# A fused convolution block of three stages: the third stage opens in an order of its own, and the taps come from eight products

## The chip, the core and the metric

One core of a Trainium2 chip. It has a matrix engine (PE, with its weight loads listed apart as PEld), a vector engine (DVE), a scalar engine for activations (ACT), GpSimd (POOL, used here for memsets and for issuing DMAs) and a queue processor that issues DMAs (SP). The program writes the order of instructions for all five by hand. The time is device microseconds of one launch; lower is better.

## What is computed

The input is x, 16 images of 192 channels and 64 × 64 pixels, f32. Layer 0 is a gated block; layer 1 is a dynamic depthwise convolution. Cut to what matters here:

```
h     = layernorm over channels (x)
p, g  = split(conv1x1(h, in_proj))                    # 192 -> 2 x 192
p     = depthwise3x3(p)
mixed = (four directional scans of p + depthwise3x3(p)) * sigmoid(g)
mixed = gelu(batchnorm(mixed))                        # mean and variance over all 16 images
x     = x + conv1x1(mixed, out_proj)                  # "out-projection", residual
h2    = layernorm over channels (x)                   # mean, variance, root
x     = x + conv1x1(gelu(conv1x1(h2, fc1)), fc2)      # 192 -> 768 -> 192
# layer 1, per image:
red   = relu(norm(mean over pixels(x) @ w1.T))        # 48 numbers
taps  = red @ w2.T + b2                               # 9 per channel, 4 of them kept by a causal mask
out   = depthwise3x3(x, taps) + bias
```

## The kernel before, in words

Stage 1 (up to about 640 us) normalises x and projects it into p and g, which go to DRAM. Stage 2 (up to about 1323 us) walks over 24 groups of 8 channels: depthwise, scans and gate, in SBUF; each finished group is stored to a DRAM tensor `mixed_d` (L707, one DMA on POOL's queue, 2 MB). The buffers for the groups take turns between `low`, `pg_o0` and `mid`. The last group lies in `mid`. Because the batch norm needs all 16 images, stage 3 can apply it only after the last group.

Stage 3 works on pairs of images, so that 64 channels of one image and 64 of the other fill 128 partitions: three "t" of 64 channels each. A pair is cut into 8 chunks of 512 pixels per image; there are 64 chunks in all. A chunk n goes through these functions:

- `load_y` (L209 to L231) reads mixed rows back for two chunks at a time: for chunks 0 and 1 into `y_low`, for chunks 2 to 7 of the first pair into parts of ximg1, the tile of the second pair's images, which isn't in use yet. With two queues it writes quarters of 64 KB (L231), with one queue larger pieces (L227).
- `unmix` (L847): three DVE transposes (`turn_back`, L239) into `mx`; `bn_gelu` (L853): batch norm and gelu on ACT, one instruction for the first two thirds (L855), one for the last (L856).
- `out_proj` (L877), for each t: four products with the last third of the channels ("quarters", L883, 64 × 64), then four with the first two thirds ("columns", L887, 128 × 64). `residual` (L890): two DVE instructions (L893) that add bias and x and write into the image tile ximg. At t = 1 and t = 2 it also adds up the channels' thirds for the mean: L897 and, by `sums`, four of L908.
- `mean` (L910, L916) turns these sums into a mean over channels by a product with a matrix of 1/192; `center` (L918, L923) subtracts it; `squares` (L927) squares on ACT (L930) and adds on DVE (L931, L908); a second `mean` makes the variance; `normalize` (L936) takes the root on ACT (L939, which needs a table load), warms up the gelu table (L941), inverts (L942) and multiplies (L943) on DVE.
- `first(n, k)` (L945), k = 0 to 2: a "hidden part", two slices of 128 hidden channels each, 24 matrix instructions a slice (L955), each slice followed by a gelu on ACT (L957). `second` (L960, by the helper `both` at L828) projects back; `final` (L969) adds.

The profile counts every f32 product as two matrix instructions with a weight load each. The matrix engine's output memory (PSUM) is laid out as two rotating tiles "f1" of two banks each, which the hidden slices, the out-projections and the means all share (in `products`, L858, a mean and an out-projection lie in two halves of the same tile), three banks "f2", and one bank "a".

When a pair is done, `pooled`, `squeeze` (L987) and `excite` (L997) make its taps. `excite` issues, for each of 3 t and 4 taps, one product for each image half (L1002, listed as L828 on the tile ps_k), and one add (L1004). The taps of pairs 0 to 6 are made between the third hidden part of a chunk and its out-projection; those of the last pair stand alone in the tail, before the last convolutions (`taps_on_diagonals`, `dynamic_last`).

The order: the loop at L1060 runs from n = -3, and in each turn touches chunk n + 3 (load, unmix, gelu), n + 2 (out-projection), n + 1 (mean to normalise), n (hidden parts) and n - 1 (the last of `second`, `final`). The first three turns have fewer members than the others. The tile pools matter as well: the pool `early` (L160), with constants, `dm` and `mid`, is closed at L795, and `k3` takes its place with ximg0 first and ximg1 behind it. With 12870 f32 per partition for each, ximg0 lies over the constants and a part of `mid`, ximg1 over the rest of `mid` and over `pg_o0`.

Of the kernel before, what the change touches and what calls it, by code (L numbers as in the profile page):

```python
# [21 lines left out]
F32 = mybir.dt.float32  # L22
AF = mybir.ActivationFunctionType
# [4 lines left out]
C = 192  # L28
HW = 64
NPIX = HW * HW  # L30
RW = HW + 2
CH = 512
HCH = CH // 2
# [22 lines left out]
def conv_block_kernel(ctx: ExitStack, tc: tile.TileContext, x, prm, w_in, w_out, w_fc1, b_fc1, w_fc2, w1, bn1, w2, out):  # L56
# [102 lines left out]

    early = ExitStack()  # L160
    ce = early.enter_context(tc.tile_pool(name="early", bufs=1))
    ones = ce.tile([128, 128], F32, tag="ones", name="ones")


# [7 lines left out]

    mats = [{"dm": ce.tile([128, 3, HW, GC], F32, tag=f"dm{i}", name=f"dm{i}")} for i in range(2)]
    mats[0]["lm"] = lm_even

    SB_ = 2 * 2 * C * BR
    mid = ce.tile([128, SB_], F32, tag="mid", name="mid")
    mats[1]["lm"] = mid[:, NPG:NPG + 5 * HW * (GC // 2)].rearrange("p (k m c) -> p k m c", k=5, m=HW)
    dev = mid[:, NPG + 5 * HW * (GC // 2):NPG + 5 * HW * (GC // 2) + 2 * C].rearrange("p (e c) -> p e c", e=2)
    lm_first = place.rearrange("p (k m c) -> p k m c", k=5, m=HW)  # L180
# [28 lines left out]
    def load_y(n, y, queues, ts=(0, 1, 2), last=32):  # L209

        p, c = divmod(n, NCH)
        for t, q, i, c0 in ((0, slice(0, 128), 0, 0), (1, slice(0, 128), 1, 0), (2, HALF[0], 0, 128), (2, HALF[1], 1, 128)):
            if t in ts:
                nq = (q.stop - q.start) // 32
                ih, i8 = divmod(2 * p + i, n_half)
                v = mixed_d[i8, c // 2, HALF[ih]].rearrange("w g e -> w (g e)")[:, c0 * BR:(c0 + 32 * nq) * BR]
                for wh in range(2):
                    vw = v[32 * wh:32 * wh + 32].rearrange("w (q e) -> q w e", q=nq)  # L220
                    qd, k = (q, wh) if t < 2 else (HALF[wh], i)
                    if last < 32:
                        for b, ncb in ((0, 32), (1, last)):
                            p0 = qd.start + 32 * b
                            queues[0].dma_start(y[p0:p0 + 32, t, k, 0:ncb * BR], vw[b, :, 0:ncb * BR])
                    elif len(queues) == 1:
                        queues[0].dma_start(y[qd, t, k], vw)  # L227
                    else:
                        for b in range(nq):
                            p0 = qd.start + 32 * b  # L230
                            queues[b % 2].dma_start(y[p0:p0 + 32, t, k], vw[b])  # L231
# [355 lines left out]
    with ExitStack() as stage:  # L587
# [100 lines left out]
        def gate(k):  # L688
            g, c = divmod(k, hp_)
            s = grp[g]  # L690
            blocks = lambda a: a.rearrange("p (n j) -> p n j", j=BR)
            for i in range(2):
                ch = c + hp_ * i

                o = s["pg"][:, :, 0, ch]
                nc.vector.tensor_mul(o, blocks(bst[k]["ps"][i]), blocks(bst[k]["sg"][i]))
                nc.vector.bn_stats(stats[:, g * GC + ch], o)
            bst[k].clear()
            if c == hp_ - 1:
                if g == NCG - 1:  # L700

                    for i in range(2):
                        for wh in range(2):
                            w0_ = 32 * wh
                            (nc.sync, nc.gpsimd)[wh].dma_start(y_low[2 * w0_ + 32:2 * w0_ + 64, 2, i, LASTC * BR:],
                                                              s["pg"][w0_:w0_ + 32, i * NB, 0].rearrange("p c j -> p (c j)"))
                nc.gpsimd.dma_start(mixed_d[:, :, :, g].rearrange("i b p e -> p (i b) e"),  # L707
                                    s["pg"][:, :, 0].rearrange("p n c j -> p n (c j)"))
                s.clear()


# [85 lines left out]


    n_img = 2
    ximg = [k3.tile([128, 3, HW + 1, RW], F32, tag=f"ximg{i}", name=f"ximg{i}") for i in range(n_img)]  # L800

    def border(xi):
        nc.gpsimd.memset(xi[:, :, 0:1], 0.0)
        nc.gpsimd.memset(xi[:, :, :, 0:1], 0.0)
        nc.gpsimd.memset(xi[:, :, :, RW - 1:RW], 0.0)
# [19 lines left out]
    def both(ps, w, rhs, start, stop):  # L825

        for i, q in enumerate(HALF):
            nc.tensor.matmul(ps[q], w(i), rhs(i), start=start, stop=stop)  # L828

    def img_of(n):  # L830
        r = 1 + (n % NCH) * CR
        return ximg[(n // NCH) % n_img][:, :, r:r + CR, 1:1 + HW]

    def rows(a):
        return a.rearrange("p (h w) -> p h w", w=HW)

    def load(n):
        if n >= 2:
            load_x2(n)
        st[n].update(x2=x2s[n % 2])  # L840
# [36 lines left out]
    def out_proj(n, t, ps):  # L877

        s = st[n]

        for wh, qr in enumerate(HALF):
            for i, q in enumerate(HALF):
                nc.tensor.matmul(ps[q, wh], wo2[qr, 64 * t:64 * t + 64], s["mx"][qr, 2, 256 * i:256 * i + 256],  # L883
                                 start=True, stop=False)
        for wh in range(2):
            for i, q in enumerate(HALF):
                nc.tensor.matmul(ps[q, wh].rearrange("p (r w) -> p r w", w=32), wo[:, 64 * t:64 * t + 64],  # L887
                                 cols(rows(s["mx"][:, i]))[:, :, wh], start=False, stop=True)

    def residual(n, t, ps):  # L890
        s, img = st[n], img_of(n)
        for wh in range(2):
            nc.vector.scalar_tensor_tensor(cols(img[:, t])[:, :, wh], ps[:, wh].rearrange("p (r w) -> p r w", w=32),  # L893
                                           pt3[:, t, OUTB:OUTB + 1], cols(rows(s["x2"][:, t]))[:, :, wh], ALU.add, ALU.add)
        if t == 1:
            s["sum"] = hp2.tile([128, 3, HCH], F32, tag="sm", name="sm", bufs=1)
            nc.vector.tensor_add(rows(s["sum"][:, 0:2].rearrange("p k n -> p (k n)")), img[:, 0], img[:, 1])  # L897
        if t == 2:
            sm = s["sum"]
            s["sm"] = [sm[:, j] for j in range(3)]  # L900
            sums(*(rows(sm[:, j]) for j in (0, 1, 2, 0, 1)), img[:, 2, 0:CR // 2], img[:, 2, CR // 2:CR])
# [8 lines left out]
    def mean(n, ps, what):  # L910


        s0, s1, sx = st[n][what]
        for k, kinds in enumerate(((s0, sx), (sx, s1))):
            for i, a in enumerate(kinds):
                nc.tensor.matmul(ps[HALF[i], k], mean64[HALF[k]], a[HALF[k]], start=True, stop=True)  # L916

    def center(n, pm):  # L918
        s, img = st[n], img_of(n)
# [76 lines left out]

    def excite(p):  # L997
        s = pst[p]
        pk = ps2.tile([128, 3, NTAP, 1], F32, tag="a", name="ps_k")
        for t in range(3):  # L1000
            for k in range(NTAP):
                both(pk[:, t, k], lambda i: w2t[:, k, 64 * t:64 * t + 64], lambda i: s["red"][:, i:i + 1], True, True)  # L1002
        taps = hp2.tile([128, 3, NTAP], F32, tag="taps", name="taps")
        nc.vector.tensor_add(taps, pk[:, :, :, 0], pt3[:, :, B2:B2 + NTAP])  # L1004
        s["taps"] = taps

    def dynamic(p, g, t):
# [42 lines left out]
    def at(f, n, *a):  # L1050
        if n is not None and 0 <= n < n_ch:
            f(n, *a)
# [4 lines left out]
        if pieces:  # L1057
            dynamic(*pieces.pop(0))

    for n in range(-3, n_ch + 1):  # L1060
        ended = (n - 1) // NCH if n >= NCH and (n - 1) % NCH == NCH - 1 else None
        if n + 5 < NCH and (n + 5) % 2 == 0:
            load_y(n + 5, ys[(n + 5) // 2], (nc.sync, nc.gpsimd) if n == -3 else (nc.gpsimd,))
        if n == -3:
            border(ximg[0])
        if n == 0:
            nc.vector.memset(pool2, 0.0)
        if n == NCH - 3:
            border(ximg[1])

        early_, late_ = (n + 3, None) if n != -1 else (None, 2)
        at(load, n + 3)
        at(unmix, early_)
        at(load_mixed, n + 4)
        at(first, n, 0)
        at(bn_gelu, early_)
        products(n, 0)
        piece()
        at(squares, n + 1)
        at(second, n - 1, NPS - 1)  # L1080
        at(final, n - 1)
        if ended is not None:
            pooled(ended)
        at(first, n, 1)
        products(n, 1)
        if ended is not None:
            squeeze(ended)
        at(second, n, 0)
# [9 lines left out]
        at(unmix, late_)  # L1098
        at(bn_gelu, late_)

    last = n_pairs - 1

# [61 lines left out]
```

## Time and profile before

| what | value |
|---|---|
| time before, median of 4 runs | 3756.06 us (3753.91 to 3762.54) |
| the profiled execution: time, span | 3753.91 us, 3752.1 us |
| PE, DVE, ACT busy, share of the span | 99%, 72%, 48% |
| first out-projection of stage 3 starts | 1330.71 us |
| first hidden part of chunk 0 starts | 1362.32 us |
| first hidden part of chunk 1 starts | 1397.44 us (chain of waits) |
| last projection ends, tail begins | 3710.4 us |

A busy share says little by itself: PE counts as busy also when it runs at half its clock, and a share is a mean over stages with different limits. The page has a row PEclk for the granted clock. Rows of groups give engine, operation, tiles written and read, shapes (partitions × elements), count, and idle time with what ended it; the timeline gives start and length in us. An "issue" as releaser means that the profile shows nothing that was waited for.

### The profile page before, as it was taken

The numbers are of one execution on the slowest core, as the hardware profiler recorded it, in microseconds if no ns is written. First come the engines' busy times: TensorE is split into PE (matmuls) and PEld (weight loads), VectorE is DVE, ScalarE is ACT, GpSimd is POOL, SyncE is SP. The second block draws the span as 40 slices with busy tenths as digits, with TensorE's granted clock in tenths as the row PEclk, the third lists the DMA queues.
The fourth block names the chain that finished last, engine by engine and source line by source line (L and its number), as shares of the span: only waits on it lengthen the run. The fifth ranks groups of instructions, "written<-read, shape, count | busy, mean of one in ns | idle before, by whom it ended". The sixth has DMA issues, their size and how long they took to land.

```text
span 3752.1 us, 71230 instructions
## 1 busy us (share of the span) xinstructions
PE 3696.8 (99%) x30252; PEld 1655.3 (44%) x30252; DVE 2716.5 (72%) x4260; ACT 1795.6 (48%) x1945; POOL 421.5 (11%) x683
## 2 busy tenths in 40 slices
PE   8999999999999979999999999999999999999998
PEld 5666656555555533333333333333333333333333
DVE  6887776999999965557756766666766776675763
ACT  3443434888888833334443434443443434443432
POOL 2334332101001020000000000000000000000000
PEclk9999999999999989999999999999999999999999
DMA  6899997999999940112222222222222221221212
GB/s 161 241 250 237 272 277 244 303 284 276 274 284 269 239 104 18 55 39 70 72 62 66 62 68 64 67 57 67 77 60 55 78 71 40 80 76 43 68 37 74
DMA packets 308429, 491.76 MB, mean 131 GB/s; under 512 B 46656, under 2 KB 202640, under 8 KB 308112
## 3 DMA queue, kind: packets, MB, share of 16 engines
q1 hardware_dynamic: 250064, 295.14, 29.8%
q0 software_dynamic: 57152, 190.94, 18.7%
q8 instruction: 239, 3.92, 0.4%
q10 hardware_dynamic: 896, 1.12, 0.1%
q14 instruction: 78, 0.64, 0.1%
HBM read 284.91 MB, written 197.92 MB: 129 GB/s over the span
## 4 chain that ended last, share of the span: by engine, by line
PE 97%; DVE 1%; DMA 1%; POOL 0%; issue 0%; ACT 0%; SPq 0%; ACTq 0%; DVEq 0%
PE ps_f L955 27%; PE ps_f L828 26%; PE ps_pj L512 13%; PE ps_l L662 11%; PE ps_d L618 7%; PE ps_o L887 5%; PE ps_xt L484 2%; PE ps_o L883 2%; PE ps_o L916 1%; DMA xa<-in_x_dram 1%; PE ps_k L828 0%; DVE v L653 0%; DVE v L655 0%; DMA ximg<-mixed_d 0%; PE ps_d L1038 0%
## 5 line engine op out<-in xcount | busy, mean ns | idle before, releaser
L957 ACT ACTIVATE gl<-ps_f,bf 128x1024 f32<-128x1024 f32 x384 | 427.9, 1114 | 1316.1 <-PE ps_f L955 1316.1
L955 PE MATMUL ps_f<-h,wf 64*64 64x512 f32 x9216 | 1036.0, 595 | 6.7 <-DVE h L943 6.6
L828 PE MATMUL ps_f<-gl,place 128*64 128x512 f32 x4608 | 1022.2, 592 | 0.0
L955 PEld LDWEIGHTS ps_f<-h,wf 64*64 64x64 f32 x9216 | 334.6, 133 | 693.8 <-issue 642.6
L828 PEld LDWEIGHTS ps_f<-gl,place 128*64 128x64 f32 x4608 | 334.2, 137 | 574.5 <-issue 533.4
L512 PE MATMUL ps_pj<-wi,xa 64*128 64x384 f32 x3072 | 516.8, 489 | 4.2 <-DVE stg L517 4.2
L923 DVE TENSOR_TENSOR h<-ximg,ps_o 128x768 f32<-128x768 f32 x128 | 116.4, 951 | 427.0 <-PE ps_o L887 418.7
L512 PEld LDWEIGHTS ps_pj<-wi,xa 64*128 64x128 f32 x3072 | 294.0, 188 | 199.0 <-issue 12.5
L893 DVE SCALAR_TENSOR_TENSOR ximg<-ps_o,pt,low 128x256 f32<-128x256 f32 x384 | 167.9, 480 | 267.4 <-PE ps_o L887 264.8
L65 DVE SCALAR_TENSOR_TENSOR o<-ximg,taps,o 128x1024 f32<-128x1024 f32 x252 | 323.3, 1283 | 8.7 <-ACT o L1014 2.6
L1018 POOL DMA_DIRECT2D out_dram<-o x168 | 88.3, 530 | 2067.2 <-DVE o L65 2064.4
L942 DVE RECIPROCAL rs<-rs 128x512 f32<-128x512 f32 x64 | 214.3, 3349 | 27.0 <-ACT rs L939 27.0
L653 DVE TENSOR_TENSOR_SCAN v<-tab,q 128x1024 f32<-128x1024 f32 x96 | 218.3, 2274 | 6.7 <-ACT tab L641 6.7
L655 DVE TENSOR_TENSOR_SCAN v<-tab,q 128x1024 f32<-128x1024 f32 x96 | 217.5, 2266 | 0.0
L518 ACT ACTIVATE stg<-ps_pj,rsa 128x384 f32<-128x384 f32 x128 | 120.1, 941 | 190.2 <-PE ps_pj L512 181.5
L887 PE MATMUL ps_o<-low,wo 128*64 128x256 f32 x1536 | 210.7, 396 | 0.0
L641 ACT ACTIVATE tab<-mask,dec_b 128x1024 f32<-128x1024 f32 x192 | 209.0, 1137 | 0.0
L518 ACT ACTIVATE mid<-ps_pj,rsa 128x384 f32<-128x384 f32 x128 | 120.6, 943 | 182.2 <-PE ps_pj L512 168.4
L491 DVE BATCH_NORM_STATS2 st<-ps_xt 128x6 f32<-128x192 f32 x512 | 174.5, 341 | 16.5 <-PE ps_xt L484 16.3
L239 DVE STREAM_TRANSPOSE low<-low 128x512 f32<-128x512 f32 x174 | 167.9, 1015 | 2.0 <-issue 0.3
L975 DVE SCALAR_TENSOR_TENSOR ximg<-ps_f,pt,ximg 128x512 f32<-128x512 f32 x192 | 134.4, 749 | 40.2 <-PE ps_f L828 37.8
L472 POOL DMA_DIRECT2D xa<-in_x_dram x192 | 120.2, 632 | 360.5 <-PE ps_pj L512 283.7
(197 smaller groups left out, 4103.7 us busy)
## 6 DMA issues: line engine op xcount, KB each, us to landing
low<-in_x_dram SPq DMA_DIRECT2D x128, 384.0 KB
out_dram<-o POOLq DMA_DIRECT2D x168, 256.0 KB, 3.7
mid<-pg_d SPq DMA_DIRECT2D x8, 4096.0 KB
low<-mixed_d SPq DMA_DIRECT2D x116, 256.0 KB
low<-pg_d SPq DMA_DIRECT2D x7, 4096.0 KB
pg_o<-pg_d SPq DMA_DIRECT2D x7, 4096.0 KB
xa<-in_x_dram POOLq DMA_DIRECT2D x192, 128.0 KB, 5.9
xa<-in_x_dram SPq DMA_DIRECT2D x192, 128.0 KB
```

The lines of the kernel that those rows point to most:

```text
L65: nc.vector.scalar_tensor_tensor(o, in0, scalar, in1, ALU.mult, ALU.add, **kw)
L512: nc.tensor.matmul(ps[i], pixels(n, t, g)[q], wi[q, t].rearrange("p g k c -> p (g k c)"), start=(t == 0), stop=(t == 2))
L518: nc.scalar.activation(stag[blk][1][:, :, j], ps[1], AF.Copy, scale=rs[:, g, 1:2])
L618: nc.tensor.matmul(dst(ps[o, ih]), mats[g % 2]["dm"][q, di + 1, :, ch], src(s["pg"][q, :, 0, ch]), start=(di == 0), stop=stop)
L653: nc.vector.tensor_tensor_scan(vf, tab, q, 0.0, ALU.mult, ALU.add)
L655: nc.vector.tensor_tensor_scan(vf[:, ::-1], tab[:, ::-1], q[:, ::-1], 0.0, ALU.mult, ALU.add)
L662: nc.tensor.matmul(dst(bst[k]["ps"][i][o]), lm_of(g)[q, m, :, c], src(q, ih), start=start, stop=stop)
L828: nc.tensor.matmul(ps[q], w(i), rhs(i), start=start, stop=stop)
L887: nc.tensor.matmul(ps[q, wh].rearrange("p (r w) -> p r w", w=32), wo[:, 64 * t:64 * t + 64], cols(rows(s["mx"][:, i]))[:, :, wh], start=Fa ...
L942: nc.vector.reciprocal(rs, rs)
L955: nc.tensor.matmul(pf[o, i], wf1[q, t, m0:m0 + 64], s["h"][q, t], start=(t == 0), stop=(t == 2))
L957: nc.scalar.activation(gl, pf, AF.Gelu, bias=bf1[:, m:m + 1])
```

## The change

Four edits. The third stage's loop starts at n = 1; what its turns -3 to 0 did is written out in a new order. In it, chunk 0's mean and variance are made without DVE sums: PE multiplies each t of the image (or of the squares) with the mean matrix and accumulates six pairs of products into a bank of its own (tag "a"). Chunk 0's out-projection takes the columns first; its square is taken in two halves, and the root's table is loaded ahead of the root by a one-column activation. `mid` becomes the first tile of `early`, and ximg1 the first of `k3`, so that ximg1 lies over `mid` (and the constants) and ximg0 over `dm` and `pg_o0`. The last group is stored in two halves, on SP and on POOL. And `excite` makes 8 products over 128 weight columns and both images' columns, then picks the right parts by four adds.

```diff
     early = ExitStack()
     ce = early.enter_context(tc.tile_pool(name="early", bufs=1))
+    SB_ = 2 * 2 * C * BR
+    mid = ce.tile([128, SB_], F32, tag="mid", name="mid")
     ones = ce.tile([128, 128], F32, tag="ones", name="ones")
...
-                nc.gpsimd.dma_start(mixed_d[:, :, :, g].rearrange("i b p e -> p (i b) e"),
-                                    s["pg"][:, :, 0].rearrange("p n c j -> p n (c j)"))
+                parts = ((nc.gpsimd, 0, n_half),) if g < NCG - 1 else ((nc.sync, 0, n_half // 2), (nc.gpsimd, n_half // 2, n_half))
+                for queue, i0, i1 in parts:
+                    queue.dma_start(mixed_d[i0:i1, :, :, g].rearrange("i b p e -> p (i b) e"),
+                                    s["pg"][:, i0 * NB:i1 * NB, 0].rearrange("p n c j -> p n (c j)"))
...
-    ximg = [k3.tile([128, 3, HW + 1, RW], F32, tag=f"ximg{i}", name=f"ximg{i}") for i in range(n_img)]
+    ximg = [k3.tile([128, 3, HW + 1, RW], F32, tag=f"ximg{i}", name=f"ximg{i}") for i in (1, 0)][::-1]
...
+    def mean_part(n, pm, t, k, src):
+        for i, q in enumerate(HALF):
+            nc.tensor.matmul(pm[q, k], mean64[q], src[q], start=(t == 0 and k == 0), stop=(t == 2 and k == 1))
...
-        pk = ps2.tile([128, 3, NTAP, 1], F32, tag="a", name="ps_k")
-        for t in range(3):
+        pk = ps2.tile([128, 2, NTAP, 2], F32, tag="a", name="ps_k")
+        for b in range(2):
             for k in range(NTAP):
-                both(pk[:, t, k], lambda i: w2t[:, k, 64 * t:64 * t + 64], lambda i: s["red"][:, i:i + 1], True, True)
+                nc.tensor.matmul(pk[:, b, k], w2t[:, k, 64 * b:64 * b + 128], s["red"], start=True, stop=True)
         taps = hp2.tile([128, 3, NTAP], F32, tag="taps", name="taps")
-        nc.vector.tensor_add(taps, pk[:, :, :, 0], pt3[:, :, B2:B2 + NTAP])
+        b2 = pt3[:, :, B2:B2 + NTAP]
+        lo, hi = HALF
+        for o, t, q, b, i in ((lo, slice(0, 2), lo, slice(0, 2), 0), (hi, slice(1, 3), hi, slice(0, 2), 1),
+                              (lo, slice(2, 3), hi, slice(1, 2), 0), (hi, slice(0, 1), lo, slice(0, 1), 1)):
+            nc.vector.tensor_add(taps[o, t], pk[q, b, :, i], b2[q, t])
...
+    load_y(2, ys[1], (nc.sync, nc.gpsimd))
+    border(ximg[0])
+    nc.vector.memset(pool2, 0.0)
+    for n in range(2):
+        load(n)
+        unmix(n)
+        bn_gelu(n)
+    hr = CR // 2
+    halves = [slice(k * hr, (k + 1) * hr) for k in range(2)]
+    img0, pm = img_of(0), one_bank()
+    for t in range(3):
+        out_alone(0, t)
+        if t:
+            for k in range(2):
+                mean_part(0, pm, t - 1, k, img0[:, t - 1, halves[k]])
+    for k in range(2):
+        mean_part(0, pm, 2, k, img0[:, 2, halves[k]])
+    center(0, pm)
+    load(2)
+    sq0 = wp.tile([128, 3, CH], F32, tag="sq2", name="sq2").rearrange("p t (k n) -> p k t n", k=2)
+    for k in range(2):
+        nc.scalar.activation(sq0[:, k], st[0]["h"].rearrange("p t (k n) -> p k t n", k=2)[:, k], AF.Square)
+    nc.scalar.activation(warm, eps6, AF.Sqrt)
+    out_alone(1, 0)
+    out_alone(1, 1)
+    pw = one_bank()
+    for k in range(2):
+        for t in range(3):
+            mean_part(0, pw, t, k, sq0[:, k, t])
+    st[0]["pw"] = pw
+    normalize(0)
+    load_y(4, ys[2], (nc.gpsimd,))
+    out_alone(1, 2)
+    first(0, 0)
+    pm = ps2.tile([128, 2, CH], F32, tag="f1", name="ps_o", bufs=2)[:, :, 0:HCH]
+    mean(1, pm, "sm")
+    unmix(2)
+    center(1, pm)
+    bn_gelu(2)
+    squares(1)
+    load(3)
+    first(0, 1)
+    unmix(3)
+    out_alone(2, 0)
+    second(0, 0)
+    bn_gelu(3)
+    products(0, 1)
+    normalize(1)
+    first(0, 2)
+    products(0, 2)
+    second(0, 1)
+
+    for n in range(1, n_ch + 1):
```

`out_alone(n, t)` is one out-projection in an f1 tile of its own with its residual, and `one_bank` a tile of tag "a". In `out_proj`, chunk 0 now issues the columns first and the quarters second, and in `residual` chunk 0 returns before the sums. From n = 1 the loop is what it was; `load_y(6)` is issued at n = 1 as before.

More of the change, by code (lines that the diff above doesn't have):

```diff
@@ L174, in conv_block_kernel @@
     mats[0]["lm"] = lm_even
-    SB_ = 2 * 2 * C * BR
-    mid = ce.tile([128, SB_], F32, tag="mid", name="mid")
     mats[1]["lm"] = mid[:, NPG:NPG + 5 * HW * (GC // 2)].rearrange("p (k m c) -> p k m c", k=5, m=HW)
@@ L879, in out_proj, with out_quarters @@
         s = st[n]
+        if n == 0:
+            out_columns(n, t, ps, True)
+            out_quarters(n, t, ps, False)
+        else:
+            out_quarters(n, t, ps, True)
+            out_columns(n, t, ps, False)
+    def out_quarters(n, t, ps, first_):
+        s = st[n]
         for wh, qr in enumerate(HALF):
@@ L883, in out_proj, with out_columns @@
                 nc.tensor.matmul(ps[q, wh], wo2[qr, 64 * t:64 * t + 64], s["mx"][qr, 2, 256 * i:256 * i + 256],
-                                 start=True, stop=False)
+                                 start=first_, stop=not first_)
+    def out_columns(n, t, ps, first_):
+        s = st[n]
         for wh in range(2):
@@ L887, in out_proj @@
                 nc.tensor.matmul(ps[q, wh].rearrange("p (r w) -> p r w", w=32), wo[:, 64 * t:64 * t + 64],
-                                 cols(rows(s["mx"][:, i]))[:, :, wh], start=False, stop=True)
+                                 cols(rows(s["mx"][:, i]))[:, :, wh], start=first_, stop=not first_)
     def residual(n, t, ps):
@@ L894, in residual @@
                                            pt3[:, t, OUTB:OUTB + 1], cols(rows(s["x2"][:, t]))[:, :, wh], ALU.add, ALU.add)
+        if n == 0:
+            return
         if t == 1:
@@ L1058, in piece, with out_alone @@
             dynamic(*pieces.pop(0))
-    for n in range(-3, n_ch + 1):
-        ended = (n - 1) // NCH if n >= NCH and (n - 1) % NCH == NCH - 1 else None
[L1062 to L1067, printed above, removed]
+    def out_alone(n, t):
+        ps = ps2.tile([128, 2, CH], F32, tag="f1", name="ps_o", bufs=2)
+        out_proj(n, t, ps[:, :, 0:HCH])
+        residual(n, t, ps[:, :, 0:HCH])
@@ new lines, in one_bank @@
+    def one_bank():
+        return ps2.tile([128, 2, HCH], F32, tag="a", name="ps_m")
+    load_y(2, ys[1], (nc.sync, nc.gpsimd))
[13 more added lines that the diff above has]
+                mean_part(0, pm, t - 1, k, img0[:, t - 1, halves[k]])
@@ new lines, in conv_block_kernel @@
+    st[0]["pw"] = pw
[21 more added lines that the diff above has]
+    for n in range(1, n_ch + 1):
+        ended = (n - 1) // NCH if n >= NCH and (n - 1) % NCH == NCH - 1 else None
+        if n == 1:
+            load_y(6, ys[3], (nc.gpsimd,))
@@ L1068, in conv_block_kernel @@
         if n == NCH - 3:
             border(ximg[1])
-        early_, late_ = (n + 3, None) if n != -1 else (None, 2)
         at(load, n + 3)
-        at(unmix, early_)
+        at(unmix, n + 3)
         at(load_mixed, n + 4)
         at(first, n, 0)
-        at(bn_gelu, early_)
+        at(bn_gelu, n + 3)
         products(n, 0)
@@ L1097, in conv_block_kernel @@
         at(second, n, 1)
-        at(unmix, late_)
-        at(bn_gelu, late_)
     last = n_pairs - 1
```

## The prediction

> **What bounds the kernel now.** I read the table by stretches first, then the order of time from 1322 to 1400 us, then the rows of the weight loads. The table's columns are busy time (and count) of PE, PEld, DVE, ACT and POOL, granted clock, DMA share, GB/s.
>
> ```profile
> 1322.00:1362.30 40.30, 20.80 (x132) 10.11 (x133) 25.61 (x43) 10.93 (x12) 20.22 (x34) 0.69 0.77 169
> 1620.00:3600.00 1980.00, 1980.00 (x15456) 735.03 (x15450) 1334.50 (x1842) 812.69 (x782) 84.06 (x160) 1.00 0.24 64
> ```
>
> In the third stage PE has no idle time at clock 1.00: a microsecond added to PE there is a microsecond of the kernel. The opening, up to 1362.3, is different: PE works 20.8 of 40.3 us, at a mean clock of 0.69, and no engine is full. It is a chain of waits, seen in the timeline (start, length, engine, line; in brackets the idle time before and what ended it):
>
> ```profile
> 1330.71 1.13 PE L883 MATMUL ps_o<-low,wo 64*64 64x256 f32 x8 [3.84 <-ACT low L856]
> 1334.87 1.66 DVE L893 SCALAR_TENSOR_TENSOR ximg<-ps_o,pt,low 128x256 f32<-128x256 f32 x4 [2.57 <-issue]
> 1335.02 5.44 SPq L231 DMA_DIRECT2D ximg<-mixed_d  x12
> ...
> 1344.14 1.82 DVE L923 TENSOR_TENSOR h<-ximg,ps_o 128x768 f32<-128x768 f32 x2 [3.83 <-PE ps_o L887]
> 1348.88 1.95 PE L916 MATMUL ps_o<-sq,mean 64*64 64x256 f32 x6 [4.79 <-DVE sq L908]
> 1355.01 1.28 ACT L939 ACT_TABLE_LOAD   x1 [7.46 <-DVE ximg L893]
> 1357.02 3.35 DVE L942 RECIPROCAL rs<-rs 128x512 f32<-128x512 f32 x1 [1.36 <-ACT rs L939]
> 1360.41 1.76 DVE L943 TENSOR_TENSOR h<-h,rs 128x1536 f32<-128x1536 f32 x1
> 1362.32 8.07 PE L955 MATMUL ps_f<-h,wf 64*64 64x512 f32 x48 [6.63 <-DVE h L943]
> ```
>
> See four things. The first residual (L893) starts at 1334.87, though its product ended at 1333.74; the first read of mixed_d starts 0.15 us later, so both waited for one thing, the landing of the last store out of `mid` (issued 1324.06, 10.7 us to landing), on which ximg0 lies. The centring (L923) waits for an out-projection that merely shares its tile. The root's table load waits for a residual (L893) for the same reason. The first hidden part takes 8.07 us where later ones take 5.31 (chain of waits), because the granted clock is 0.50 until 1367.8 (table in steps of 1 us).
>
> **The opening.** Prices at full clock are from the chain: out-projection of one t 0.43 + 1.01 = 1.44; at half clock 1.13 + 1.90 = 3.03. A pair of direct mean products on two diagonal quarters has no row: from below 0.43 (L916 and L883 run four quarters, two steps, in that), from above 0.51 (half of L887's 1.01, four steps). I take 0.50, so 1.0 per t and 3.0 for a whole mean; the lower end saves 0.9 in all.
>
> Chunk 0, in the trace's clock. The columns now go first, so PE needs only the first gelu (ends 1329.95): t=0 runs 1330.0 to 1332.96 at half clock, t=1 to 1334.75 (the clock rose at 1333.67 in the trace). Mean of t=0 to 1335.75, t=2 to 1337.2, mean of t=1 to 1338.2. Residual t=2 (0.88) is done by 1338.2, mean of t=2 ends 1339.25. Each residual is hidden by the next product. Centring (1.82) 1339.4 to 1341.2; the two half squares, 0.9 each (L930 is 1.48 for the double), end at 1342.2. Meanwhile PE does chunk 1's t=0 and t=1 to 1342.1. Variance: six pairs, 1345.1. Three DVE groups of before are gone from this chain: sums 0.69 + 1.77, sums of squares 0.69 + 1.77. The root's table load (1.28) now runs beside the variance. From root to first product the trace takes 1362.32 − 1356.30 = 6.02 us, and nothing of that changes: 1345.25 + 6.02 = **1351.3, 11.0 earlier**. Chunk 1's t=2 covers only 1.44 of the wait, so PE idles 4.7 us and cools. In the trace the clock changed at 1333.67, 1340.5 and 1354.1, multiples of 3.41 us apart, so the cold part of the next product is 2.9 or 6.3 us: it takes 6.7 or 8.4; I take 7.5.
>
> From there to chunk 1's first product (1397.44 in the chain of before), PE's order is: mean 0.43, a wait of 0.75 for the second gelu (1.11) to give back its bank, 5.31, 1.44, 5.15, 1.87, 5.31 with a wait of 0.45 (its second half needs the bank that root 1 reads, behind the residual and a table load), 1.44, 5.15. That is 27.3 against 27.05 before. Arrival 1386.1 instead of 1397.4: **−11.4 us**. Ends: −9 with the colder product and the upper prices, −14 with the better ones.
>
> Covers. On DVE, the unmixing of chunk 2 (three times 1.0) stands ahead of chunk 1's centring; it is free from 1353.9 and may start as late as 1357.9, since the fourth hidden slice needs the centred bank at 1362.7. It needs the rows that SP and POOL read from 1335.0; POOL's quarters landed 3.1 us after issue (median), the last was issued by 1341.5, so some 12 us of cover remain. Its gelu stands on ACT before two others; that slips past PE only after 1360.7. x2 of chunks 2 and 3 is loaded at the same place of SP or earlier; the memset of pool2 (0.06) runs under the transposes. POOL's order (read, borders, two reads) does not change.
>
> **The tile and the store.** ximg0 no longer lies on `mid`, so the residual starts with its product, 1333.05; the second image's rows, which do lie on it, wait as before. If the wait stays after all (a residual after the landing, at the latest 1334.87), mean t=0 begins 1.0 later: +1.0. Half of the store goes to SP, behind L705 and ahead of the reads, which wait for the landing anyway. DMA share was 0.95 to 1.01 from 1327 to 1333.5, so the split cannot shorten the transfer, only bring forward some of POOL's 1.75 us of issue. I cost it at nothing: what waits for the landing now are only the reads, with the cover above.
>
> **The taps.** 24 products in halves (48 instructions) become 8 over all columns (16), and one add becomes four.
>
> ```profile
> 1683.61 1.45 PE L828 MATMUL ps_k<-red,w2t 48*64 48x1 f32 x46
> 98.66 1.12 PEld L341 LDWEIGHTS pb<-pt,place 64*64 64x64 f32 x18 [0.55 <-issue]
> 636.94 4.30 PEld L140 LDWEIGHTS pb_h<-pt,wf 64*128 64x128 f32 x36 [1.72 <-ACT mid L518]
> 1192.57 0.96 PEld L735 LDWEIGHTS pq<-ones,stats 128*128 128x128 f32 x4 [0.74 <-DVE stats L697]
> 3712.86 2.72 PE L828 MATMUL ps_k<-red,w2t 48*64 48x1 f32 x48 [0.62 <-DVE red L994]
> ```
>
> These rows are from the timeline. Each product has one column to multiply, so the spacing is the weight load. On one quarter 64 columns take (1.12 − 0.13)/17 = 0.058 us (L341). The taps' two halves alternate and come at 0.028: they overlap in pairs. L140 loads 128 contiguous columns and needs (4.30 − 0.19)/35 = 0.117, or about 0.107 in its stretches at clock 1.00. So fewer instructions are not less time. Before, the taps push PE's next product back by 6.47 − 5.20 = 1.27 (from the start of a hidden part to the out-projection behind it, with taps between at 1678.41, without at 1641.55). New, 16 × 0.11 = 1.76: **+0.49 each, +3.4 for seven pairs**. PE is full there, so nothing hides it. The last pair runs at clock 0.50 in the tail: 16 × 0.22 = 3.52 against 2.72, +0.8, and three more adds at 0.17 are +0.5, as both taps on diagonals and ACT wait: **+1.3**. With x for one load at full clock, taps cost 7(16x − 1.27) + 32x − 2.2. From below x is 0.056 (both halves at once, at the pace of the taps' pairs), from above 0.24 (L735, four in 0.96); I take L140, nearest in shape: contiguous, 128 columns, one column multiplied.
>
> [...]
>
> **Sum.** −11.4 + 3.4 + 1.3 = −6.7. The profiled execution took 3753.91 (span 3752.1, 1.8 around it): 3747.2. It is the lowest of four runs, 2.15 under their median of 3756.06, partly perhaps for its clock; the new opening has fewer cold stretches, so I leave the sum where it is. Against the median it is −8.9, or 0.24%.
>
> **Rivals.**
> Opening gains less: the residual still waits (+1.0), cold windows fall worse (+1.5), small waits between engines (+0.1 to 0.2 at some ten new hand-overs). That is 3749.5 to 3753, for: no row shows this order; against: each cover has slack.
> Taps get cheaper: all columns load in one pair's time, x = 0.056, taps −3.0: 3753.91 − 14.4 = 3739.5. For: halves do overlap; against: L140.
> Slower: the 128-wide loads run at L735's 0.24. Seven pairs cost 7 × 2.57 = +18, the tail +5.5, in all +12: 3766. It decides at x = 0.156, where the sum is zero. Against: L735's columns lie six elements apart, those of w2t side by side, like L140's.
> The change doesn't do what it says: chunk 2's rows land late and the unmixing blocks centring. Each microsecond after 1357.9 costs one. But the trace's unmixing at 1364.80 started without waiting, so at most 6.9: 3754.
>
> **Chances.** Forecast 0.55 (its own range 3744 to 3750), opening gains less 0.20, cheap taps 0.15, late rows 0.04, slow loads 0.06. The range 3739 to 3752.5 leaves out the last two and a part of the second. About 0.2% (7.5 us) is what a measurement tells from no change; that bound, 3748.5, cuts the forecast: faster 0.50 (0.35 of the forecast, all cheap taps), same 0.44, slower 0.06.
>
> **What would show it.** Right: first hidden part near 1351; sixteen tap products spread over 1.7 to 1.8 us at full clock; residual t=0 within 0.2 us of its product; no DVE idle before the unmixing of chunk 2. Wrong: tap products under 1.2 us; a store landing that ends the first residual's wait; PE at half clock between 1334 and 1346.

## The result and the profile after

| | before | after |
|---|---|---|
| median | 3756.43 us, 55 runs | 3760.73 us, 34 runs |
| profiled execution: span | 3752.1 us | 3759.4 us |
| first hidden part of chunk 0 | 1362.32 us | 1357.45 us |
| first hidden part of chunk 1 | 1397.44 us | 1393.37 us |

The changed kernel is slower by 0.12%: ratio 1.0012, 95% interval 1.0007 to 1.0017. A gain of 0.24% was forecast, with an upper end of 3752.5 us, so the time is outside the range and on the other side of no change. Five single slow executions, at 3829 to 8995 us (two of the kernel before, one each of e1, e2 and e3), are left out of the medians and ratios of the experiments.

Start with the table of stretches of the kernel after. The columns are those of the prediction: busy time and count of PE, PEld, DVE, ACT and POOL, granted clock, DMA share, GB/s.

```profile
1322.00:1362.30 40.30, 26.06 (x188) 12.94 (x192) 27.63 (x45) 13.30 (x16) 17.54 (x31) 0.71 0.77 160
...
1620.00:3600.00 1980.00, 1980.00 (x15140) 735.19 (x15140) 1333.68 (x1859) 807.88 (x778) 84.06 (x160) 1.00 0.23 64
```

The opening did become denser: PE works 26.06 of the same 40.30 us instead of 20.80. In the long stretch PE is still full. Its clock is printed as 1.00, and three short drops are rounded away in that number; they come up below.

Next, the timeline of the kernel after, around the first out-projection (start, length, engine, line; in brackets the idle time before and what ended it):

```profile
1330.62 1.05 DVE L239 STREAM_TRANSPOSE low<-low 128x512 f32<-128x512 f32 x1 [0.31 <-issue]
...
1335.44 1.03 DVE L239 STREAM_TRANSPOSE low<-low 128x512 f32<-128x512 f32 x1 [3.77 <-issue]
1335.46 0.06 DVE L1099 MEMSET pool<- 128x6 f32 x1
1335.65 5.43 SPq L231 DMA_DIRECT2D ximg<-mixed_d  x12
1336.18 5.91 POOL L231 DMA_DIRECT2D ximg<-mixed_d  x12 [8.81 <-DMA mixed_d<-mid]
1336.40 1.92 DVE L239 STREAM_TRANSPOSE low<-low 128x512 f32<-128x512 f32 x2
1337.43 1.24 ACT L858 ACTIVATE low<-low,bn_bi,bn_sc 128x1024 f32<-128x1024 f32 x1 [4.64 <-DVE low L239]
1338.25 1.61 DVE L909 SCALAR_TENSOR_TENSOR ximg<-ps_o,pt,low 128x256 f32<-128x256 f32 x4
...
1339.18 1.88 PE L939 MATMUL ps_m<-ximg,mean 64*64 64x256 f32 x8 [2.03 <-issue]
```

Read it from the middle. DVE does one transpose and then nothing for 3.77 us, with "issue" as the releaser: the profile names nobody there. Then a memset and a transpose start within 0.02 us of each other, and 0.2 and 0.7 us later SP and POOL start to read `mixed_d`, POOL with its releaser written out: the landing of the last store from `mid`. So I read that the memset of pool2 (L1099) was waiting for that landing; moving it is the test below. It stands on DVE ahead of chunk 1's three transposes, and behind these stand the first residuals (L909). They start at 1338.25; the first one's product had ended by 1335.2. PE then idles 2.03 us ahead of the first mean.

Last, the chain of waits of the kernel after at two places where taps are made (start, length, engine, tile, line). L978 is a hidden part, L1026 the taps, L896 and L903 the out-projection, L831 the `second`.

```profile
1679.72 1.87 PE ps_k L1026 x16
1681.60 0.59 PE ps_o L896 x8
1682.19 1.01 PE ps_o L903 x8
1683.20 5.15 PE ps_f L831 x24
1688.35 5.31 PE ps_f L978 x48
...
1974.70 1.87 PE ps_k L1026 x16
1976.57 0.59 PE ps_o L896 x8
1977.16 1.44 PE ps_o L903 x8
1978.60 6.42 PE ps_f L831 x24
1985.02 5.31 PE ps_f L978 x48
```

The same 16 tap products take 1.87 us in both (1.29 before, for 48). But in the second pair the work after them is longer: 1.44 instead of 1.01, 6.42 instead of 5.15. From taps to next hidden part that is 8.63 and 10.32 us; before, all seven pairs took 8.00. Four pairs are of the first kind and three of the second. The table of stretches of the same kernel shows why (the clock is third from the end):

```profile
1974.70:1976.60 1.90, 1.90 (x20) 1.88 (x24) 0.00 (x0) 1.11 (x1) 0.00 (x0) 1.00 0.00 0
1976.60:1978.00 1.40, 1.40 (x16) 0.68 (x18) 0.65 (x4) 0.00 (x0) 0.00 (x0) 0.86 0.00 0
1978.00:1980.00 2.00, 2.00 (x8) 0.68 (x6) 1.29 (x3) 0.00 (x0) 0.00 (x0) 0.50 0.00 0
1980.00:1982.00 2.00, 2.00 (x10) 0.72 (x8) 1.90 (x4) 0.00 (x0) 0.00 (x0) 0.74 0.45 120
1982.00:1985.00 3.00, 3.00 (x20) 0.78 (x14) 2.33 (x3) 0.00 (x0) 0.00 (x0) 1.00 0.82 182
```

PE counts as busy without a gap, yet its clock is at half from 1977.6 to 1981.0, one stretch of 3.4 us that begins 1 us after the tap burst.

**The span accounted for.** S below is the start of the last statistics instruction of stage 2 (L697, or L698 where lines were added above it), the last point up to which the two programs do the same. S is 1322.68 before and 1324.82 after: +2.1, of a stage that was not changed. From S to the first mean over pixels of a chunk (ps_t, a landmark behind the opening): 350.37 and 344.16, −6.2. Seven pairs of taps: 7 × 0.63 + 3 × 1.70 = +9.5. Tail, from the last ps_t on: 40.29 and 42.06, +1.8. The sum is +7.2 of the +7.3 us of the spans.

### The profile page after: what moved, and what is told of

It is laid out like the page before. It is cut to its first block, busy times and chain, and to the rows that moved or that the text cites. A ratio compares the mean times of both kernels' runs of the same rounds, so it can differ in the third digit from the quotient of the medians.

```text
span 3759.4 us, 70799 instructions
## 1 busy us (share of the span) xinstructions
PE 3708.3 (99%) x30028; PEld 1727.6 (46%) x30028; DVE 2714.3 (72%) x4274; ACT 1795.0 (48%) x1947; POOL 421.0 (11%) x683
## 4 chain that ended last, share of the span: by engine, by line
PE 96%; DMA 2%; DVE 1%; issue 0%; ACT 0%; SPq 0%; POOL 0%; ACTq 0%; DVEq 0%
PE ps_f L978 27%; PE ps_f L831 26%; PE ps_pj L512 13%; PE ps_l L662 11%; PE ps_d L618 6%; PE ps_o L903 5%; PE ps_xt L484 2%; PE ps_o L896 2%; PE ps_o L934 1%; DMA xa<-in_x_dram 1%; PE ps_k L1026 0%; DMA pg_d<-mid 0%; DVE v L653 0%; DVE v L655 0%; PE ps_d L1066 0%
## 5 line engine op out<-in xcount | busy, mean ns | idle before, releaser
L978 PE MATMUL ps_f<-h,wf 64*64 64x512 f32 x9216 | 1036.2, 595 | 5.7 <-DVE h L966 4.6
L831 PE MATMUL ps_f<-gl,place 128*64 128x512 f32 x4608 | 1026.2, 594 | 0.0
L978 PEld LDWEIGHTS ps_f<-h,wf 64*64 64x64 f32 x9216 | 334.5, 133 | 692.7 <-issue 640.8
L831 PEld LDWEIGHTS ps_f<-gl,place 128*64 128x64 f32 x4608 | 335.4, 137 | 577.9 <-issue 537.2
L909 DVE SCALAR_TENSOR_TENSOR ximg<-ps_o,pt,low 128x256 f32<-128x256 f32 x384 | 167.9, 480 | 262.0 <-PE ps_o L903 258.3
L903 PE MATMUL ps_o<-low,wo 128*64 128x256 f32 x1536 | 211.5, 397 | 3.1 <-ACT low L858 3.1
```

The source lines that it names most:

```text
L978: nc.tensor.matmul(pf[o, i], wf1[q, t, m0:m0 + 64], s["h"][q, t], start=(t == 0), stop=(t == 2))
```

## The experiments

Two theories were put against each other at each place. Opening: the memset's wait holds it, or the landing holds it through the image tile itself, whatever stands first. Taps: the wide products cost their loads alone, or the clock answers to them as well. One table for all runs, in us; ratios are against the kernel before, with their 95% interval. "Opening" is S to first ps_t; "first residual" is counted from S; "taps" is from the taps to the next hidden part, for the seven pairs.

| kernel | ratio | opening | first residual | taps | tail |
|---|---|---|---|---|---|
| before | 1 | 350.37 | 12.19 | 8.00 × 7 | 40.29 |
| after | 1.0012 [1.0007, 1.0017] | 344.16 | 13.43 | 8.63 × 4, 10.33 × 3 | 42.06 |
| e1_old_taps | 0.9978 [0.9968, 0.9988] | 342.08 | 13.41 | 8.00 × 7 | 38.97 |
| e2_new_taps_alone | 1.0026 [1.0017, 1.0035] | 348.51 | 12.21 | 8.63 × 4, 10.32 × 3 | 42.01 |
| e3_memset_later | 1.0012 [1.0001, 1.0022] | 339.86 | 10.68 | 8.63 × 4, 10.33 × 3 | 40.6 |
| e4_two_pools | 0.9997 [0.9988, 1.0006] | 338.98 | 10.44 | 8.63 × 3, 10.33 × 4 | 41.01 |
| e5_taps_in_two | 0.9984 [0.9975, 0.9993] | 340.07 | 10.44 | 8.87 × 7 | 40.24 |
| e6_taps_twice | one run, 3791.5 us | 339.44 | 10.42 | 13.6 to 13.7 × 5, 12.0 × 2 | 42.82 |
| e7_two_pools_old_taps | 0.9974 [0.9965, 0.9982] | 339.81 | 10.43 | 8.00 × 7 | 38.59 |
| e8_twelve_narrow | 0.9955 [0.9942, 0.9968] | 338.82 | 10.44 | 7.30 × 7 | 38.7 |
| e9_old_tile_order | one run, 3764.64 us | 338.66 | 10.67 | 8.63 × 3, 10.33 × 4 | 41.86 |
| e10_one_store | one run, 3758.57 us | 340.99 | 12.19 | 8.63 × 4, 10.32 × 3 | 41.74 |

**The taps undone, and alone.** The kernel after with the products of before:

```diff
-        pk = ps2.tile([128, 2, NTAP, 2], F32, tag="a", name="ps_k")
-        for b in range(2):
+        pk = ps2.tile([128, 3, NTAP, 1], F32, tag="a", name="ps_k")
+        for t in range(3):
             for k in range(NTAP):
-                nc.tensor.matmul(pk[:, b, k], w2t[:, k, 64 * b:64 * b + 128], s["red"], start=True, stop=True)
+                both(pk[:, t, k], lambda i: w2t[:, k, 64 * t:64 * t + 64], lambda i: s["red"][:, i:i + 1], True, True)
...
+        nc.vector.tensor_add(taps, pk[:, :, :, 0], pt3[:, :, B2:B2 + NTAP])
```

> The changed kernel with the 24 narrow tap products of before. Theory (the opening gains about 6 us, the taps lose about 11): about 6 us faster than before, near 3750, tap products 1.3 us per pair and no drop of the granted clock behind them. Rival (the opening itself loses, the taps cost only the forecast +4.7): about equal to before, 3756 or more.

And the reverse, the kernel before with the wide products and nothing else:

> The kernel before with the 8 wide tap products and nothing else of the change. [...] Rival (forecast's price, loads only): +4.7, 3761, and no pair at half clock.

The wide taps are the loss. Without them the changed kernel takes 3749.41 us, 0.22% less than the kernel before; alone they cost 0.26%. They bring the same 8.63 and 10.32, four pairs and three, into the old order, with no change of opening or store: seven times 0.63 and three times 1.7 for the pairs, where loads alone were priced at 0.49 a pair. The timed runs show the clock's part too: the mean granted clock is 0.9919 over 35 runs of the kernel after and 0.9942 over nine of e1, and 0.0023 of 3757 us is 8.8 us more lost to the clock. In e2 the opening is of the same program as before and yet 1.9 us shorter: PE's clock is at half for 30.7 us of it before and for 26.0 in e2. After and e1, which also open alike, differ by 2.1. So an opening in a single profile is known to about 2 us.

**The memset behind the residuals.**

```diff
-    nc.vector.memset(pool2, 0.0)
     for n in range(2):
...
     out_alone(1, 1)
+    nc.vector.memset(pool2, 0.0)
     pw = one_bank()
```

> The changed kernel with the memset of pool2 moved behind the residuals of chunk 1's first two t. Theory (the first DVE write into the closed pool's room waits for the last store's landing, whoever makes it): chunk 1's transposes start right after chunk 0's last, the first residual waits for the landing instead, the first hidden part comes 1.5 to 3 us earlier relative to the last statistics: 3758 to 3759. Rival (the transposes themselves wait, or chunk 1's rows are late): the transposes stay where they are, no change.

DVE's timeline in this kernel:

```profile
1333.90 3.82 DVE L239 STREAM_TRANSPOSE low<-low 128x512 f32<-128x512 f32 x4 [0.31 <-issue]
...
1338.76 0.88 DVE L909 SCALAR_TENSOR_TENSOR ximg<-ps_o,pt,low 128x256 f32<-128x256 f32 x2 [1.04 <-DMA mixed_d<-mid]
```

The transposes go through in one piece. The wait has not gone: it has passed to the first residual, and now the profile names it, the landing of the store. Both theories were right in part. In both kernels the landing's wait is held by the first DVE write into the new pool; with the memset it held three transposes and a gelu too. The opening falls from 344.16 to 339.86 (from 342.08 in e1). The 1.5 to 3 us that were expected of it did not come in the time: the ratio stays at 1.0012, though its interval reaches down to 1.0001. This is the one timed run whose pieces do not explain it (see below).

**Two pools, so that the first image does not lie on the stored tile's pool.**

```diff
     mid = ce.tile([128, SB_], F32, tag="mid", name="mid")
+    ce = early.enter_context(tc.tile_pool(name="early2", bufs=1))
...
+    k3a = ctx.enter_context(tc.tile_pool(name="k3a", bufs=1))
...
-    ximg = [k3.tile([128, 3, HW + 1, RW], F32, tag=f"ximg{i}", name=f"ximg{i}") for i in (1, 0)][::-1]
+    ximg = [p_.tile([128, 3, HW + 1, RW], F32, tag=f"ximg{i}", name=f"ximg{i}") for i, p_ in ((1, k3a), (0, k3))][::-1]
```

The memset stays where the run before put it, here and in all runs that follow.

> As the run with the later memset, and in addition `mid` and ximg1 in pools of their own, so that the room of ximg0 is released without the last store. Theory (release goes by pool, not by tile, which is why the tile swap bought nothing): the first residual starts within 0.3 us of its product and the first hidden part 28 to 30 us after the last statistics begin (32.6 in the changed kernel): 3 to 4.5 us faster than the changed kernel, about 3756. Rival (release goes by tile): same as the run with the later memset.

The first residual in DVE's timeline of this kernel:

```profile
1332.59 0.88 DVE L911 SCALAR_TENSOR_TENSOR ximg<-ps_o,pt,low 128x256 f32<-128x256 f32 x2 [0.81 <-PE ps_o L898]
```

Now its own product releases it. With S taken off, that is 0.24 us earlier than in e3, so once the memset is out of the way the landing costs the first residual almost nothing. The opening is 338.98, which is 11.4 less than before: the forecast's term to the tenth, where one program's own openings differ by 2, so the tenth is luck. Its landmarks agree as well: chunk 0's first hidden part starts at S + 28.86 (the forecast's 1351.3 is S + 28.6), chunk 1's at S + 63.37 (1386.1 is S + 63.4). Whether the pools are worth more than that 0.24 is not settled: the intervals of e3 and e4 overlap. Those of e4 and the kernel after do not: later memset and pools together are worth 0.15% with the wide taps.

**The old order of the tiles**, with `mid` last in `early` and ximg0 first in `k3`, on e3:

```diff
-    ximg = [k3.tile([128, 3, HW + 1, RW], F32, tag=f"ximg{i}", name=f"ximg{i}") for i in (1, 0)][::-1]
+    ximg = [k3.tile([128, 3, HW + 1, RW], F32, tag=f"ximg{i}", name=f"ximg{i}") for i in range(n_img)]
```

> As the run with the later memset, but with the order of tiles of before (`mid` late in its pool, ximg0 ahead of ximg1). Theory (release goes by pool): the swap of tiles does nothing, the first residual starts 10.6 to 10.8 us after the last statistics begin, as with the swap. Rival (the swap frees ximg0): the residual comes later than 11.5 us, or moves in some other way by over 0.5 us.

The first residual is at S + 10.67, against 10.68 in e3. The swap of the tiles, one of the four edits of the change, does nothing for that wait (one execution each). With e4, where a pool of its own ended the wait, it follows that here room is given back by the pool, not by the tile, and both images lie in one pool.

**One store**, on e3, with the last group on POOL's queue alone:

```diff
-                parts = ((nc.gpsimd, 0, n_half),) if g < NCG - 1 else ((nc.sync, 0, n_half // 2), (nc.gpsimd, n_half // 2, n_half))
+                parts = ((nc.gpsimd, 0, n_half),)
```

> As the run with the later memset, but the last group is stored by one DMA on POOL's queue as before. Theory (the wait is the landing of that store, and the split brings it forward): the first residual starts 12.1 to 12.3 us after the last statistics begin, as in the kernel before, 1.5 us later than with the split. Rival (the transfer is bound by bandwidth and the split brings nothing, as forecast): 10.7 us.

DVE's timeline:

```profile
1337.90 1.66 DVE L909 SCALAR_TENSOR_TENSOR ximg<-ps_o,pt,low 128x256 f32<-128x256 f32 x4 [2.56 <-issue]
```

S + 12.19, the very number of before. So the split brought the landing forward by 1.5 us (12.19 − 10.68), and DVE waits 2.56 instead of 1.04. It did so by starting the transfer earlier, not by shortening it: in steps of 1 us from S, the DMA share is 0.97 to 1.02 from the fifth to the eleventh step with one store, and with two it is 0.65 in the third, 0.95 to 1.11 from the fourth to the ninth and 0.84 in the tenth. The opening is 1.1 longer than in e3, which is within what one program's openings differ by.

**Half of the wide products before the out-projection, half behind it**, on e4. If it is the whole burst of 1.87 us that costs the clock, no pair drops here; if something else at that place of the chunk does, three or four of seven drop, as in the kernels with the whole burst:

```diff
-            excite(ended)
+            excite(ended, 0)
...
+        if ended is not None:
+            excite(ended, 1)
```

> Base: the run with two pools. The eight wide tap products are issued as four ahead of the out-projection and four behind it. [...]

The chain of waits in this kernel:

```profile
1678.16 0.98 PE ps_k L1028 x8
1679.14 0.59 PE ps_o L898 x8
1679.73 1.01 PE ps_o L905 x8
1680.75 0.98 PE ps_k L1028 x8
1681.73 5.30 PE ps_f L833 x24
```

The same loads, two bursts of 0.98, and no drop in any of seven pairs: 8.87 each, 0.24 above a whole burst without a drop.

**Each wide product twice**, on e4 (`for b in (0, 1, 0, 1)`; the second pass writes the same values again). If the length of the burst counts, more pairs than e4's four drop; if it does not, a pair costs only the 1.87 of the added loads:

> Base: the run with two pools; every wide tap product is issued twice (the second overwrites the first with the same numbers). [...]

The chain of waits:

```profile
1982.46 3.76 PE ps_k L1028 x32
1986.22 1.06 PE ps_o L898 x8
1987.28 1.90 PE ps_o L905 x8
1989.19 5.28 PE ps_f L833 x24
```

All seven pairs drop, five of them, at 13.6 to 13.7, for two stretches of 3.4 us; the other two, at 12.0, for one. Over the seven pairs the second pass costs 3.6 us each against e4, where its loads alone are 1.87.

**The old products on the good opening**, e4 with the edit of e1:

> Two pools and the 24 narrow tap products of before: the opening as forecast and no loss at the taps. Theory: opening 10 to 11 us better than before, nothing lost later: 3745 to 3748, 0.25 to 0.3% faster than before. Rival (openings vary from run to run and the gain is given back later in the stage): 3750 or more.

3746.64 us: the opening's gain with nothing given back, and almost the forecast's number, though not by the forecast's change. Against e1, which has these taps behind the opening with the early memset, the time is only 0.04% lower and the intervals overlap: with these taps the timing does not resolve what the later memset and the pools are worth (openings 342.08 and 339.81).

**Twelve narrow products**, on e4: 64 columns per product, so that neighbours go to alternating halves of the columns, and both images' columns in one product; four adds pick the parts.

```diff
-        pk = ps2.tile([128, 2, NTAP, 2], F32, tag="a", name="ps_k")
-        for b in range(2):
+        pk = ps2.tile([128, 3, NTAP // 2, 2], F32, tag="a", name="ps_k")
+        for t in range(3):
             for k in range(NTAP):
-                nc.tensor.matmul(pk[:, b, k], w2t[:, k, 64 * b:64 * b + 128], s["red"], start=True, stop=True)
+                nc.tensor.matmul(pk[HALF[k % 2], t, k // 2], w2t[:, k, 64 * t:64 * t + 64], s["red"], start=True, stop=True)
...
+        for i, o in enumerate(HALF):
+            for h, q in enumerate(HALF):
+                nc.vector.tensor_add(taps[o, :, h::2], pk[q, :, :, i], b2[q, :, h::2])
```

> Two pools and another form of the taps: 12 products over 64 weight columns, both images' columns at once, on alternating halves of the array, and four adds. Theory (64-column loads on alternating halves come every 0.028 us): 24 x 0.028 = 0.67 us instead of 1.32, 0.6 us a pair less than the 24 narrow products, no clock drop, and +0.5 - 0.7 to -1.3 in the tail: 4 to 6 us faster than the run with 24, near 3742. Rival (the pace is set by something else than the loads, the number of results for one): 1.2 us or more a pair, equal to the run with 24.

The chain of waits, where the 24 instructions of the products are now 0.59 us:

```profile
1669.27 0.59 PE ps_k L1027 x21
...
1670.40 1.01 PE ps_o L905 x8
1671.41 5.15 PE ps_f L833 x24
```

3737.69 us, the fastest of all and 4 us better than expected (five executions): 0.45% below the kernel before (interval 0.32% to 0.58%), from −11.6 in the opening, −0.70 for each of seven pairs, −1.6 in the tail.

**Do the pieces make the times?** Opening, taps and tail against the kernel before, then the timed difference (ratio less one, times 3757), in us: after +5.1 and +4.5; e1 −9.6 and −8.3; e2 +9.3 and +9.8; e4 +0.5 and −1.1; e5 −4.3 and −6.0; e7 −12.3 and −9.8; e8 −18.1 and −16.9. All of these lie inside the interval of their ratio. Only e3 stands apart, −0.7 against +4.5 (interval +0.4 to +8.3). The number of drops changes from run to run, and each is 1.70, but the mean granted clock is 0.9922 over e3's ten runs and 0.9926 over e4's eleven, so the clock can account for some 1.5 us of the 5. Stage 2 also ends at another time in each execution (last section). What made e3 slow stays open.

## Why the prediction was wrong

**The first step that failed, and the larger: the taps at "+0.49 each, +3.4 for seven pairs".** The load price was nearly right. The burst took 1.87 for 16, 0.117 each (0.11 was taken), and a pair without a drop costs +0.63. What failed is that the price was the loads' alone. The sentence "PE is full there, so nothing hides it" treated a PE that is full as a PE whose clock stays up. The prediction had used the same clock, with its steps of 3.41 us, in the opening, and did not ask what it does behind 1.87 us of loads. Three pairs of seven paid 1.70 more: +9.5 in all, not +3.4. No rival had it; the slow rival gave a wrong mechanism (0.24 per load) for the right side.

The row that the price came from ("I take L140, nearest in shape") shows the same thing. L140's 36 loads run from 636.94 to 641.24 in the kernel before, and the table of stretches there says:

```profile
639.00:640.00 1.00, 1.00 (x11) 1.00 (x11) 0.00 (x0) 0.00 (x0) 1.00 (x3) 1.00 0.65 148
640.00:641.00 1.00, 1.00 (x11) 1.00 (x10) 0.00 (x0) 0.00 (x0) 0.24 (x1) 0.88 0.55 88
641.00:642.00 1.00, 1.00 (x6) 0.58 (x10) 0.16 (x1) 0.00 (x0) 0.00 (x0) 0.50 0.86 262
```

PE is busy without a gap, each product has one column, and 3.8 us into the burst the clock falls to half. In all twelve profiles it falls inside this burst, 1.2 to 3.9 us after its start. The prediction wrote "about 0.107 in its stretches at clock 1.00" beside its price and did not ask why the row had other stretches. The number itself is low: there are 28 loads in the 3.00 us from 637 to 640 only with those that reach into it; from start to start the 34 loads from 636.9 to 640.6, all at clock 1.00, are 0.112 apart.

**The other step that failed: "the memset of pool2 (0.06) runs under the transposes".** It was priced by its length, and its wait was not looked for, though its tile comes from a pool that lies on what is stored last. The opening gained 6.2 instead of 11.4 in this profile, and 8.3 in e1, which opens alike; with the later memset and the split store it gained 10.3 to 11.7. The profiles put the price of that wait at 2 to 5 us. The timed runs show it only together with the pools (0.15%, e4 against after). "ximg0 no longer lies on `mid`, so the residual starts with its product" failed with it: the wait belongs to the pool (e9 against e3). The hedge for a wait that stays after all, +1.0, was too small by its place, because it let the residual alone wait; what waited stood ahead of three transposes and a gelu.

**Right.** The opening's term: with that wait out of the way, seven kernels with the split store gained 10.3 to 11.7 and the eighth, with one store, 9.4, against −11.4 with ends of −9 and −14. The tail's two terms: a burst of 3.58 at half clock (3.52 forecast) and four adds in 0.70 (one took 0.17). That the tail as a whole came to +1.8 against +1.3 is partly luck: the chain of waits has the diagonal products behind it at 9.92 instead of 8.73, under one more stretch at half clock, and tails with the same taps differ by up to 1.7 us between profiles. The unmixing of chunk 2 was not late, and the rival of late rows did not come up.

**Mis-costed without consequence.** Half of the store on SP, at "nothing": it brings the landing 1.5 us forward (e10 against e3). The reason given, that the split cannot shorten the transfer but only bring it forward, holds. The price counts wherever something waits for the landing.

**In the sum**, 5.2 missing in the opening, 6.1 more for the taps and 0.5 in the tail are 11.8: from −6.7 to +5.1, against +4.5 timed. These are the pieces of one profiled execution. Without the three drops, or without the shortfall of the opening, they would add up to about nothing. The forecast of 0.24% also counted 2.15 us by which the profiled execution lay under its group's median; its sum alone, −6.7, is 0.18%.

## What to carry to other kernels

Where a matrix engine is full, ask of every inserted group of products what the clock does behind it, not only how long it takes: here a burst of 1.87 us of weight loads with two columns each cost up to 1.70 us more in the clock behind it, and its halves, placed apart, lost no clock. Price an instruction that opens a new tile by what its room waits for, and then by everything queued behind it on its engine; a memset of 0.06 us held 3.77 here. And when an edit moves a wait, look at which instruction inherits it.

## What was not expected of the hardware

**In these profiles the clock falls on a grid of 3.4133 us.** The drops after tap bursts begin at 1977.60, 2274.57 and 3455.57 us in the kernel after: the differences, 296.97 and 1181.0, are 87 and 346 times 3.4133. In the six kernels with the eight wide products in one burst (after, e2, e3, e4, e9, e10) I laid such a grid under all 42 bursts in the loop, for each kernel from one of its own drops. The 20 whose first product began 0.10 to 0.84 us into a stretch of the grid were followed by a drop; the 22 that began from 1.24 to 3.37 us into one were not. Shorter bursts began in that same early part too (their grids laid from drops in the tail): five bursts of 24 narrow products (1.29 us, in before, e1 and e7), three halves of e5 (0.98) and six bursts of e8 (0.59). None of them was followed by a drop. So here both the length and the place count. The share of loads in a stretch does not settle it: in a stretch with a drop behind it the burst fills 1.87 of 3.41 us, 55%, but six bursts that began at 1.24 to 1.39 also lie whole inside their stretch and were not followed by a drop. What in a burst or around it the clock answers to was not shown.

**Fewer instructions, more time.** The loads of the taps in the kernel after (first the whole kernel by length, then one pair in the timeline), and the same for one pair of e8:

```profile
L1026 PEld LDWEIGHTS ps_k<-red,w2t x128: 182/188/330, 1679.7 to 3721.5; 48*128 48x128 f32 x128
1679.65 1.86 PEld L1026 LDWEIGHTS ps_k<-red,w2t 48*128 48x128 f32 x16 [0.81 <-issue]
```

```profile
L1027 PEld LDWEIGHTS ps_k<-red,w2t x24: 133/135/135, 1668.7 to 1669.7; 48*64 48x64 f32 x24
1669.10 0.67 PEld L1027 LDWEIGHTS ps_k<-red,w2t 48*64 48x64 f32 x20 [0.29 <-issue]
```

The lengths (minimum, median, maximum in ns) overlap and do not add up. What counts is the pace from start to start: (1.86 − 0.19)/15 = 0.111 us for 128 columns, (0.67 − 0.13)/19 = 0.028 us for 64 on alternating halves. Twice the columns cost four times as much, which I read as neighbours on different halves overlapping where full-width loads do not.

**An unchanged stage moves the time by more than the change.** S was between 1319.7 and 1339.0 us in twelve profiled executions, all of the same stages 1 and 2. Single executions that differ by a few us say nothing of an edit in stage 3; differences from S say more, down to the 2 us by which one program's openings differ.
